# A six-block decoder on one core: the low-rank pieces ahead of ScalarE's transfers, and the second causal attention divided by GpSimd

## The chip, the core and the metric

The kernel runs on one core of a Trainium2 chip. The core has TensorE (PE in the profile; its weight loads are PEld), VectorE (DVE), ScalarE (ACT), GpSimd (POOL) and SyncE (SP), which here only starts transfers. ScalarE starts transfers as well, and each queue of transfers stands in line with what its engine does: a row marked ACTq or SPq is time of that engine's queue. The metric is the device time of one execution in microseconds, as a median of several runs; lower is better.

## The reference

The input is x of 8 batches x 128 tokens x 512 features, with a context of the same shape. Six blocks follow each other, and behind each one the result is added to x and layer-normalized:

```python
x = _layernorm(x + _L0_attn_ref(...))      # causal attention, 32 heads of 16
x = _layernorm(x + _L0_xattn_ref(...))     # autocorrelation with the context (FFT, top 9 lags)
x = _layernorm(x + _L0_ffn_ref(...))       # base matrix + low-rank experts, 2 of 28 by a router
x = _layernorm(x + _L1_attn_ref(...))      # causal attention with ALiBi, q and k layer-normalized
x = _layernorm(x + _L1_xattn_ref(...))     # cross attention: 16 heads of 96, 4 key heads
x = _layernorm(x + _L1_ffn_ref(...))       # 8 low-rank heads of rank 16, mixed by a softmax
```

The change touches the fourth block and the seam between the fifth and the sixth. The fourth, cut to what matters:

```python
qkv = jnp.clip(jnp.einsum('bsd,ed->bse', hidden_states, Wqkv), -8.0, 8.0)
q, k, v = jnp.split(qkv, [D_MODEL, 2 * D_MODEL], axis=-1)
q = _layer_norm(q, q_ln_w, q_ln_b)         # weights and biases over the 512 features
k = _layer_norm(k, k_ln_w, k_ln_b)
scores = jnp.einsum('bqhd,bkhd->bhqk', q, k) * scale + slopes * rel   # causal
probs = jax.nn.softmax(scores, axis=-1)
out = jnp.einsum('bhqk,bkhd->bqhd', probs, v)
return jnp.einsum('bsd,ed->bse', out, Wout)
```

The sixth block is `2 * sum over h of softmax(x Wr + br)[h] * 8 * (x A[h]) B[h]`.

## The kernel before

Everything is float32. Tokens of one batch stand on the 128 partitions; transposes that a product needs are made on TensorE against an identity. The program is written once as straight code. A planner then orders each engine's instructions: by their place in the program, but among those that by its own cost estimates are ready. So an instruction can run ahead of one written before it. `tc.issue_after` pins an order by hand. Waits between engines are put in by the framework.

**Second causal attention** (tiles named `..._a`, lines 164 to 240 and 600 to 860). The loop runs over the batches b, and in each over f = 0 and 2, half of the heads. One such step makes a `Heads16`: scores on TensorE (L164), the ALiBi bias and the maxima on VectorE (L672, L181), exponentials on ScalarE in two halves `exps(0)` and `exps(1)` (L193, each with its sum into `su`). The steps overlap three deep: while step n is scored, `turn` turns the exponentials of step n-1 on TensorE (`pt`, L212; copied by VectorE and ScalarE, L213), and `out` multiplies those of step n-2 with the values (L229, L235). The softmax's division is made at the end: `turn` takes the reciprocals of the sums (L202, `rc`), GpSimd spreads them over the features (L205, `rb`), TensorE turns them too (`pr`, L218), ScalarE copies them (`rT`, L220), and `out` multiplies its result with them on VectorE (L240). Beside that the next batch's q, k and v are made (`normed`, `values`): clipped and normalized by VectorE (L627, L631; the root of the variance by GpSimd, L97), multiplied by the norm's weights and raised by its biases on GpSimd (L632, L633), from `lnv`, four rows broadcast to all partitions whose q part is scaled once (L611). Then `turned_both` turns q (a VectorE copy, L137) and k (into `kbd`, which keeps two heads apart, L657).

**Cross attention and low-rank block** (tiles named `..._x`, lines 780 to 1150). Per batch there are two steps hh = 0, 1 of a `Heads8`: scores (L876), maxima, exponentials (L897), division and 32x32 transposes on VectorE (L904, L905), and then `turn`, 16 transfers from SBUF to SBUF that finish the transpose into `pT` (L911). `outputs(b)` multiplies with the values (`mixed`, L921) and `projected(b)` projects (L938) and normalizes. The pieces of the low-rank block run beside this: `low_tokens` (transposes of x), `low_scores` (products, L951, and the router's softmax, L960 to 973, with one exponential on ScalarE), `low_turn` (one transpose `pt_lT` on TensorE and one ScalarE copy `lT`, L1003 and L1006), `low_last` (a product `pof`, L1011, a normalization and the transfer of the output from SP, L1016). `nxt.go(n)` lets n pieces of the next pair's front part (token transposes, value products `pvx`, key products `pkx`, query products `pqx`) be issued.

For batches 0 to 5 all transfers of `turn` are started by SP. For the last two batches they are started together at the end of hh = 1, alternately by SP and ScalarE:

```python
                    pTs[b] = pT_tile(b)
                    for heads in (first, now):
                        heads.turn(pTs[b], (nc.sync, nc.scalar))
```

`pT` has one buffer, so these transfers wait until the values product of the batch before has read it. The buffers `e` of a `Heads8` are two, so the exponentials two steps later wait for the transfers that read the same buffer. The scores of one `Heads8` fill both pairs of PSUM banks in that pool, so the next scores wait for its exponentials.

Of the kernel before, what the change touches and what calls it, by code (L numbers as in the profile page):

```python
# [43 lines left out]
def decoder(ctx: ExitStack, tc: tile.TileContext, a: dict, out: bass.AP):  # L44
# [101 lines left out]
    class Heads16:  # L146
# [7 lines left out]

        W = 3 * P

        def __init__(self, pool, units, bias, o_dst, name, between=()):
            self.pool, self.units, self.o_dst, self.name = pool, units, o_dst, name
# [38 lines left out]

        def turn(self):


            rc = sm.tile([P, 16], F32, tag="rc", name=f"rc_{self.name}")
            nc.vector.reciprocal(rc, self.su.rearrange("p a r x -> p (a r x)"))  # L202

            rb = self.pool.tile([P, 2, 8, HD], F32, tag="rb", name=f"rb_{self.name}", bufs=1)
            nc.gpsimd.tensor_copy(rb, bc(rc.rearrange("p (a h) -> p a h", a=2).unsqueeze(3), [P, 2, 8, HD]))  # L205
            self.pT = self.pool.tile([P, 4, self.W], F32, tag="pT", name=f"pT_{self.name}", bufs=1)
            for i in range(2):
                pt = banks(f"pt_{self.name}_{i}")
                for r in range(2):
                    for k in range(3):  # L210
                        cols = slice(k * P, (k + 1) * P)
                        nc.tensor.transpose(pt[:, r, cols], self.e[:, 2 * i + r, cols], ident)  # L212
                (nc.scalar.copy if i else nc.vector.tensor_copy)(  # L213
                    self.pT[:, 2 * i : 2 * i + 2, :], pt[:, :, : self.W]
                )
            pr = bank(f"pr_{self.name}")
            for a in range(2):
                nc.tensor.transpose(pr[:, a * P : (a + 1) * P], rb[:, a].rearrange("p h d -> p (h d)"), ident)  # L218
            self.rT = self.pool.tile([P, 2, P], F32, tag="rT", name=f"rT_{self.name}", bufs=1)
            nc.scalar.copy(self.rT, pr[:, : 2 * P].rearrange("p (a q) -> p a q", a=2))  # L220

        def out(self):
            o = bank(f"o_{self.name}")
            for u, (_, _, v, vd) in enumerate(self.units):
# [9 lines left out]
                for r in range(4):  # L234
# [4 lines left out]
                    )  # L239
            nc.vector.tensor_tensor(  # L240
# [367 lines left out]
    lnv = kp.tile([P, 4, D], F32, tag="lnv", name="lnv")  # L608
    nc.sync.dma_start(lnv, a["L1_ln"].partition_broadcast(P))

    nc.gpsimd.tensor_scalar(lnv[:, 0:2, :], lnv[:, 0:2, :], SCALE, None, ALU.mult)  # L611
# [8 lines left out]
    def normed(i, b, xT, later=None):  # L620
# [9 lines left out]
        def normalized():  # L630
            done = nc.vector.tensor_scalar(q, q, mean, rs, ALU.subtract, ALU.mult)  # L631
            nc.gpsimd.tensor_tensor(q, q, lnv[:, 2 * i, :], ALU.mult)  # L632
            nc.gpsimd.tensor_tensor(q, q, lnv[:, 2 * i + 1, :], ALU.add)  # L633
# [16 lines left out]
    def turned_both(b, q, k):  # L650
        qT = ap.tile([P, NC, P], F32, tag="qT", name=f"qT1_{b}")
        transposed(q, NC, P, qT, f"qT1_{b}", "v")
# [5 lines left out]
        return qT, kbd  # L658
# [68 lines left out]
    qk = turned_both(0, *raw)  # L727
# [73 lines left out]
    for b in range(B):  # L801
# [3 lines left out]
        for f in (0, 2):  # L805
# [4 lines left out]
            now = Heads16(ap, units, alibi_bias(f), oT[:, f : f + 2, :], f"a1_{b}_{f}", keys_late)  # L810
            now.exps(0)
# [15 lines left out]
            if prev:  # L827
                prev.turn()
            now.exps(1)
            half = projection(b - 1, oT_before) if f == 2 and b else iter((0, 0))  # L830
            next(half)
            if b + 1 < B:
                if f == 0:
                    raw.append(normed(1, b + 1, xT, keys_late))
                else:
                    qk = turned_both(b + 1, *raw)
# [17 lines left out]
    with stage("x1b", 2, side="right") as ap, stage("f1", 2, side="right") as fp:  # L854
# [206 lines left out]
        for b in range(B):  # L1061
# [4 lines left out]
            for hh in range(2):  # L1066
# [4 lines left out]
                if b < B - 2 and hh == 0:  # L1071

                    nxt.go(3 if b < B - 3 else 2)
# [4 lines left out]
                elif b < B - 2:  # L1078
# [7 lines left out]
                    if b < B - 3:  # L1086
                        nxt.go(2)
# [7 lines left out]
                else:  # L1095
                    if b == B - 1:
                        low_turn(B - 4)
                        low_tokens(B - 3)
                    outputs(b - 1)
                    pTs[b] = pT_tile(b)  # L1100
                    for heads in (first, now):
                        heads.turn(pTs[b], (nc.sync, nc.scalar))
                    if b == B - 2:
                        low_turn(B - 5)
                        low_scores(B - 4)
                        low_last(B - 5)
            vs_x[b] = front.v[:, j]

        low_last(B - 4)
        projected(B - 2, {3: [lambda: low_scores(B - 3)]})  # L1110
        weight_sums()
        low_turn(B - 3)
        outputs(B - 1)
# [102 lines left out]
def _layouts(i):  # L1216
# [18 lines left out]
        ),  # L1235
        "L1_ln": np.stack([i[f"L1_attn_{k}"] for k in ("q_ln_w", "q_ln_b", "k_ln_w", "k_ln_b")]),
# [49 lines left out]
```

## Time and profile before

| what | value |
|---|---|
| median of 3 runs | 893.53 us (892.61 to 895.29) |
| the profiled execution | 892.05 us, its span 890.2 us |
| mean granted TensorE clock | 0.991 |
| busy: TensorE, VectorE, ScalarE, GpSimd | 852.1, 565.4, 362.0, 166.3 us |
| first causal attention and autocorrelation | to about 230 us |
| experts, beside the rest of the autocorrelation | to about 330 us |
| second causal attention | about 330 to 510 us |
| cross attention and low-rank block | about 510 to 890 us |

A row of the timeline gives start, duration, engine, line, operation, the tiles written and read, the shape, how many, and in brackets how long the engine had been idle and what ended that. A row of a group gives the busy time, the mean in ns, and the idle time ahead of it with the engines that ended it.

### The profile page before, as it was taken

What the parts mean: (1) busy time and instruction counts of PE and PEld (TensorE: products, weight loads), DVE (VectorE), ACT (ScalarE), POOL (GpSimd) and SP (SyncE); (2) the same over time, 40 slices, a digit from 0 to 9 for tenths busy, and PEclk for the clock granted to TensorE, in tenths of its full rate; (3) what the DMA queues carried; (4) which work ended last, traced back from release to release, by engine and by line L of the source; (5) the groups of instructions that cost most, each with busy time, mean ns of one, the idle gap of its engine ahead of it and who ended that gap; (6) DMA issues with size and microseconds to landing.
All of it is one profiled execution on the core that took longest, in us unless ns stands there. A gap on an engine that the chain in (4) does not pass through costs nothing.

```text
span 890.2 us, 16965 instructions
## 1 busy us (share of the span) xinstructions
PE 852.1 (96%) x6486; PEld 527.7 (59%) x6486; DVE 565.4 (64%) x1321; ACT 362.0 (41%) x1518; POOL 166.3 (19%) x235
## 2 busy tenths in 40 slices
PE   9999999899899999999999999999999999995996
PEld 5766655654455455555556687857485847582442
DVE  3756797786968667888888513724462546465644
ACT  3787474664223116666666502305030403053200
POOL 2500233132433313333333000000000000000000
PEclk9999999999999999999999999999999999998998
DMA  9800000130300002000004020432232222224040
GB/s 322 328 2 25 2 13 13 49 108 1 154 1 24 1 0 96 2 1 1 2 2 143 26 72 1 92 74 48 48 72 48 61 48 60 48 60 95 18 102 35
DMA packets 29921, 51.19 MB, mean 58 GB/s; under 512 B 5392, under 2 KB 21904, under 8 KB 27920
## 3 DMA queue, kind: packets, MB, share of 16 engines
q1 hardware_dynamic: 27280, 48.01, 18.1%
q10 hardware_dynamic: 2560, 2.10, 1.1%
q8 instruction: 51, 0.84, 0.4%
q14 instruction: 30, 0.25, 0.1%
HBM read 31.21 MB, written 2.10 MB: 37 GB/s over the span
## 4 chain that ended last, share of the span: by engine, by line
PE 68%; DVE 16%; ACT 9%; SPq 2%; issue 2%; ACTq 1%; POOL 1%; DMA 1%; POOLq 0%; DVEq 0%
PE pox L938 10%; PE pqx L86 6%; ACT e_a L193 5%; PE pq L86 5%; PE pkx L86 5%; PE pk L86 4%; PE pv L86 4%; PE pof L86 4%; PE o_x L921 3%; PE pt_a L212 3%; PE s_x L876 3%; PE pvx L86 3%; PE po L665 2%; PE s_a L164 2%; SPq L911 2%
## 5 line engine op out<-in xcount | busy, mean ns | idle before, releaser
L193 ACT ACTIVATE e_a<-e_a,m_a 128x128 f32<-128x128 f32 (+1 forms) x512 | 184.9, 365 | 113.8 <-DVE m_a L181 113.8
L897 ACT ACTIVATE e_x<-s_x,m_x 128x256 f32<-128x256 f32 x128 | 58.6, 483 | 135.8 <-DVE m_x L887 125.2
L193 ACT ACTIVATION_READ_ACCUMULATOR e_a<-e_a,m_a 128x1 f32 x512 | 97.6, 191 | 0.0
L938 PE MATMUL pox<-w_X_o,oTx 128*128 128x512 f32 x192 | 86.3, 604 | 0.0
L86 PE MATMUL pqx<-xTx,w_X_q 128*128 128x256 f32 x384 | 84.9, 380 | 0.0
L86 PEld LDWEIGHTS pqx<-xTx,w_X_q 128*128 128x128 f32 x384 | 72.6, 190 | 11.4 <-issue 1.8
L886 DVE TENSOR_REDUCE m_x<-s_x 128x4 f32<-128x1024 f32 x32 | 37.6, 1216 | 43.4 <-PE s_x L876 43.4
L938 PEld LDWEIGHTS pox<-w_X_o,oTx 128*128 128x128 f32 x192 | 36.6, 194 | 48.2 <-issue 47.7
L181 DVE TENSOR_REDUCE m_a<-e_a 128x4 f32<-128x512 f32 (+1 forms) x128 | 62.6, 543 | 0.0
L212 PE MATMUL pt_a<-ident,e_a 128*128 128x128 f32 x384 | 48.6, 274 | 4.9 <-DVE e_a L352 3.9
L212 PEld LDWEIGHTS pt_a<-ident,e_a 128*128 128x128 f32 x384 | 43.4, 140 | 12.8 <-DVE e_a L352 4.9
L97 POOL TENSOR_TENSOR rs_x<-ve_x,neghalf 128x1 f32<-128x1 f32 x7 | 3.8, 548 | 251.0 <-DVE ve_x L95 251.0
L876 PE MATMUL s_x<-kTx,qTx 32*128 32x256 f32 x768 | 46.1, 383 | 0.0
L921 PE MATMUL o_x<-pT_x,vx 128*32 128x512 f32 x384 | 43.3, 595 | 1.5 <-DVE oTx L927 1.4
L876 PEld LDWEIGHTS s_x<-kTx,qTx 32*128 32x128 f32 x768 | 38.1, 185 | 9.9 <-issue 7.4
L103 DVE TENSOR_TENSOR x_x<-pox,x_a 128x512 f32<-128x512 f32 x7 | 4.8, 692 | 56.5 <-PE pox L938 56.5
L905 DVE STREAM_TRANSPOSE e_x<-e_x 128x1024 f32<-128x1024 f32 x32 | 39.7, 1241 | 0.8
L904 DVE TENSOR_SCALAR e_x<-e_x,rc_x 128x256 f32<-128x256 f32 x128 | 36.4, 347 | 3.5 <-DVE rc_x L901 2.3
L164 PEld LDWEIGHTS s_a<-kbd,qT 32*64 32x64 f32 x1024 | 20.7, 131 | 28.1 <-issue 8.9
L792 ACT COPY qTx<-pqx 128x512 f32<-128x512 f32 x24 | 14.1, 594 | 55.5 <-PE pqx L86 55.5
L164 PE MATMUL s_a<-kbd,qT 32*64 32x256 f32 (+1 forms) x1024 | 33.3, 335 | 1.8 <-DVE pT_a L213 0.8
L202 DVE RECIPROCAL rc_a<-su_a 128x16 f32<-128x16 f32 x32 | 8.0, 251 | 40.6 <-ACT e_a L193 40.6
(222 smaller groups left out, 1637.7 us busy)
## 6 DMA issues: line engine op xcount, KB each, us to landing
pT_x<-e_x SPq DMA_DIRECT2D x224, 64.0 KB, 2.0
w_X_q<-in_X_q SPq DMA_DIRECT2D x3, 1024.0 KB, 4.8
w_X_o<-in_X_o SPq DMA_DIRECT2D x3, 1024.0 KB, 4.9
w_L_Wv<-in_L_Wv SPq DMA_DIRECT2D x2, 1024.0 KB, 6.4
w_L_Wo<-in_L_Wo SPq DMA_DIRECT2D x2, 1024.0 KB, 7.9
x_in<-in_x SPq DMA_DIRECT2D x8, 256.0 KB, 7.5
ct<-in_ctx SPq DMA_DIRECT2D x8, 256.0 KB, 4.4
cT<-in_ctxT SPq DMA_DIRECT2D x4, 512.0 KB, 3.9
```

What stands on the lines that cost most here:

```text
L86: nc.tensor.matmul(ps, lhsT=l, rhs=r, start=(i == 0), stop=(i == n - 1))
L164: nc.tensor.matmul(s[r // 2][64 * u : 64 * u + 64, r % 2, cols], lhsT=qT[rows, 64 - 64 * part : P - 64 * part], rhs=kbd[rows, :, :keys], s ...
L181: self.scored = nc.vector.tensor_reduce(self.m[:, part, rs, :], self.by_heads(part)[:, rs], AX.X, ALU.max, negate=True)
L193: nc.scalar.activation(e[:, r, x, :], e[:, r, x, :], AF.Exp, bias=self.m[:, part, r, x : x + 1], accum_out=self.su[:, part, r, x : x + 1],)
L212: nc.tensor.transpose(pt[:, r, cols], self.e[:, 2 * i + r, cols], ident)
L876: nc.tensor.matmul(sc[g // 2][:, g % 2, u * 256 : (u + 1) * 256], lhsT=qT[rows, (h0 + u) * NS + n, :], rhs=kT[rows, n], start=(n == 0), st ...
L886: nc.vector.tensor_reduce(m, self.s[i], AX.X, ALU.max, negate=True)
L897: nc.scalar.activation(self.e[:, :, j, :], self.s[half][:, i, :].rearrange("p (a k) -> p a k", k=32), AF.Exp, bias=self.m[:, j : j + 1], s ...
L904: nc.vector.tensor_scalar(e, e, self.rc[:, j : j + 1], None, ALU.mult)
L905: nc.vector.transpose(self.e[:, :, js, :], self.e[:, :, js, :])
L921: nc.tensor.matmul(po[32 * g : 32 * g + 32, :], lhsT=v[:, s, g * XD + 32 * n : g * XD + 32 * n + 32], rhs=pT[:, s].rearrange("p i h x -> p ...
L938: nc.tensor.matmul(po, lhsT=oT[:, n, h * P : (h + 1) * P], rhs=w, start=(i == 0), stop=(i == NX - 1))
```

## The change

1. In the second causal attention `divide(half)` takes the reciprocals of a half's sums as soon as its exponentials are made, and GpSimd multiplies the exponentials by them in place, before they are turned. The spread, the turn and the copy of the reciprocals leave `turn`; `out` copies instead of multiplying.
2. The norm of the queries is finished behind the transpose: ScalarE copies the turned queries feature by feature with the norm's weight as scale and its bias as addend. GpSimd's two operations on q go. The queries of the next batch are turned behind the scores of f = 2, the keys stay where they were. `lnv` keeps the keys' two rows, and `lnq` is a small tile for the queries.
3. In the last two batches the pieces of the low-rank block that stood behind the transfers, or behind the values product, are issued ahead of them. At the end `outputs(B - 1)` stands ahead of `low_turn(B - 3)`.
4. The front pieces of the even batches are shared out as 4 + 2 + 1 instead of 3 + 2 + 2.

```diff
+        def divide(self, half):
+            rs = slice(2 * half, 2 * half + 2)
+            if self.rc is None:
+                self.rc = sm.tile([P, 2, 4, 2], F32, tag="rcd", name=f"rc_{self.name}")
+            nc.vector.reciprocal(self.rc[:, :, rs, :], self.su[:, :, rs, :])
+            for part in range(2):
+                e = self.by_heads(part)[:, rs]
+                nc.gpsimd.tensor_tensor(e, e, bc(self.rc[:, part, rs, :].unsqueeze(3), list(e.shape)), ALU.mult)
+
         def turn(self):
-            rc = sm.tile([P, 16], F32, tag="rc", name=f"rc_{self.name}")
-            nc.vector.reciprocal(rc, self.su.rearrange("p a r x -> p (a r x)"))
...
+            if self.rc is None:
+                rc = sm.tile([P, 16], F32, tag="rc", name=f"rc_{self.name}")
...
+            if self.rc is not None:
+                return
             pr = bank(f"pr_{self.name}")
...
+            if self.rc is not None:
+                nc.vector.tensor_copy(self.o_dst, o[:, : 2 * P].rearrange("p (u q) -> p u q", u=2))
+                return
             nc.vector.tensor_tensor(
...
-    lnv = kp.tile([P, 4, D], F32, tag="lnv", name="lnv")
-    nc.sync.dma_start(lnv, a["L1_ln"].partition_broadcast(P))
-
-    nc.gpsimd.tensor_scalar(lnv[:, 0:2, :], lnv[:, 0:2, :], SCALE, None, ALU.mult)
+    lnv = kp.tile([P, 2, D], F32, tag="lnv", name="lnv")
+    nc.sync.dma_start(lnv, a["L1_ln"][2:4].partition_broadcast(P))
+    lnq = kp.tile([P, 2, NC], F32, tag="lnq", name="lnq")
+    nc.sync.dma_start(lnq, a["L1_lnq"])
+    nc.gpsimd.tensor_scalar(lnq, lnq, SCALE, None, ALU.mult)
...
-            nc.gpsimd.tensor_tensor(q, q, lnv[:, 2 * i, :], ALU.mult)
-            nc.gpsimd.tensor_tensor(q, q, lnv[:, 2 * i + 1, :], ALU.add)
+            if i:
+                nc.gpsimd.tensor_tensor(q, q, lnv[:, 0, :], ALU.mult)
+                nc.gpsimd.tensor_tensor(q, q, lnv[:, 1, :], ALU.add)
...
-    def turned_both(b, q, k):
+    def turned_queries(b, q):
         qT = ap.tile([P, NC, P], F32, tag="qT", name=f"qT1_{b}")
-        transposed(q, NC, P, qT, f"qT1_{b}", "v")
+        pt = bank(f"pTq1_{b}")
+        for c in range(NC):
+            nc.tensor.transpose(pt[:, c * P : (c + 1) * P], q[:, c * P : (c + 1) * P], ident)
+        for c in range(NC):
+            nc.scalar.activation(
+                qT[:, c, :], pt[:, c * P : (c + 1) * P], AF.Identity, scale=lnq[:, 0, c : c + 1], bias=lnq[:, 1, c : c + 1]
+            )
+        return qT
+
+    def turned_keys(b, k):
...
+            if f == 2 and b + 1 < B:
+
+                qT = turned_queries(b + 1, raw[0])
             now.exps(0)
             catch_up(now.scored)
...
+            now.divide(0)
             now.exps(1)
...
-                    qk = turned_both(b + 1, *raw)
+                    qk = qT, turned_keys(b + 1, raw[1])
+            now.divide(1)
...
-                    nxt.go(3 if b < B - 3 else 2)
+                    nxt.go((4, 3)[j] if b < B - 3 else 2)
...
-                        nxt.go(2)
+                        nxt.go((1, 2)[j])
...
                 else:
+                    low_turn(b - 3)
                     if b == B - 1:
-                        low_turn(B - 4)
                         low_tokens(B - 3)
                     outputs(b - 1)
+                    if b == B - 2:
+                        low_scores(B - 4)
+                    low_last(b - 3)
+
                     pTs[b] = pT_tile(b)
                     for heads in (first, now):
                         heads.turn(pTs[b], (nc.sync, nc.scalar))
-                    if b == B - 2:
-                        low_turn(B - 5)
-                        low_scores(B - 4)
-                        low_last(B - 5)
             vs_x[b] = front.v[:, j]
 
-        low_last(B - 4)
         projected(B - 2, {3: [lambda: low_scores(B - 3)]})
         weight_sums()
+        outputs(B - 1)
         low_turn(B - 3)
-        outputs(B - 1)
         low_tokens(B - 2)
         low_last(B - 3)
```

More of the change, by code (lines that the diff above doesn't have):

```diff
@@ L157, in __init__ @@
         def __init__(self, pool, units, bias, o_dst, name, between=()):
-            self.pool, self.units, self.o_dst, self.name = pool, units, o_dst, name
+            self.pool, self.units, self.o_dst, self.name, self.rc = pool, units, o_dst, name, None
             s = [banks(f"s_{name}_{i}") for i in range(2)]
@@ L196, in exps @@
                         )
-        def turn(self):
-            rc = sm.tile([P, 16], F32, tag="rc", name=f"rc_{self.name}")
-            nc.vector.reciprocal(rc, self.su.rearrange("p a r x -> p (a r x)"))
-            rb = self.pool.tile([P, 2, 8, HD], F32, tag="rb", name=f"rb_{self.name}", bufs=1)
-            nc.gpsimd.tensor_copy(rb, bc(rc.rearrange("p (a h) -> p a h", a=2).unsqueeze(3), [P, 2, 8, HD]))
+        def divide(self, half):
[6 more added lines that the diff above has]
+                nc.gpsimd.tensor_tensor(e, e, bc(self.rc[:, part, rs, :].unsqueeze(3), list(e.shape)), ALU.mult)
+        def turn(self):
+            if self.rc is None:
+                rc = sm.tile([P, 16], F32, tag="rc", name=f"rc_{self.name}")
+                nc.vector.reciprocal(rc, self.su.rearrange("p a r x -> p (a r x)"))
+                rb = self.pool.tile([P, 2, 8, HD], F32, tag="rb", name=f"rb_{self.name}", bufs=1)
+                nc.gpsimd.tensor_copy(rb, bc(rc.rearrange("p (a h) -> p a h", a=2).unsqueeze(3), [P, 2, 8, HD]))
             self.pT = self.pool.tile([P, 4, self.W], F32, tag="pT", name=f"pT_{self.name}", bufs=1)
@@ L657, in turned_both @@
         nc.vector.tensor_tensor(kbd, bc(pt.unsqueeze(1), [P, 2, D]), bc(pair.unsqueeze(2), [P, 2, D]), ALU.mult)
-        return qT, kbd
+        return kbd
     def projection(b, oT):
@@ L726, in decoder @@
     xT = turned_tokens(1)
-    qk = turned_both(0, *raw)
+    qk = turned_queries(0, raw[0]), turned_keys(0, raw[1])
     E(6)
@@ L1235, in _layouts @@
         ),
+        "L1_lnq": np.stack([cols(i[f"L1_attn_{k}"]) for k in ("q_ln_w", "q_ln_b")], axis=1),
         "L1_ln": np.stack([i[f"L1_attn_{k}"] for k in ("q_ln_w", "q_ln_b", "k_ln_w", "k_ln_b")]),
```

## The prediction

> **What bounds the kernel now.** I read the page's rows by slice first, then TensorE's waits over the last stage, then the timelines of TensorE and ScalarE around its one long wait, then the chain of waits in the second causal layer, and last the rows of single operations.
>
> ```profile
> PE   9999999899899999999999999999999999995996
> PEclk9999999999999999999999999999999999998998
> POOL 2500233132433313333333000000000000000000
> PE pof L1011 <- ACT lT L1006: 9.7, 2, 9.3
> PE o_x L921 <- DVE oTx L927: 1.4, 2, 0.7
> PE pt_lT L1003 <- DVE ve_x L95: 1.0, 1, 1.0
> ```
>
> TensorE (PE) is busy nearly everywhere. The dent in slice 37 is one wait of 9.3 us: the low-rank product of batch 3 (pof) waits for ScalarE's copy of the turned low-rank piece (lT).
>
> ```profile
> 808.47 2.87 PE L876 MATMUL s_x<-kTx,qTx 32*128 32x256 f32 x48
> 820.61 2.08 PE L1011 MATMUL pof<-wf,lT 128*128 128x512 f32 x2 [9.26 <-ACT lT L1006]
> 822.48 12.14 PE L938 MATMUL pox<-w_X_o,oTx 128*128 128x512 f32 x24
> 834.55 2.87 PE L876 MATMUL s_x<-kTx,qTx 32*128 32x256 f32 x48
> 808.96 11.21 ACTq L911 DMA_DIRECT2D pT_x<-e_x  x14
> 820.28 0.28 ACT L1006 ACTIVATE lT<-pt_lT 128x128 f32<-128x128 f32 x1 [11.44 <-DMA pT_x<-e_x]
> 837.77 0.28 ACT L1006 ACTIVATE lT<-pt_lT 128x128 f32<-128x128 f32 x1 [13.30 <-PE pt_lT L1003]
> ```
>
> The copy takes 0.28 us, but stands behind 16 transfers that ScalarE starts for batch 6 (807.42 to 820.17). The last line is the same copy one batch on: there low_turn stands ahead of the transfers in the program, and the copy runs 6 us before them (they start at 843.82).
>
> ```profile
> 401.53 1.31 PE pt_a L212 x12
> 402.84 0.22 PE pr_a L218 x2
> 403.05 3.44 PE pk L86 x8
> 406.49 0.84 PE s_a L164 x32
> ```
>
> In the second causal layer the chain of waits is TensorE without a gap, 21.79 us a batch (scores at 396.25 and 418.04); its two steps hold one pr_a each.
>
> **The change, part by part.** The sum is made against the profiled execution: 892.05 us, its span 890.2 and 1.85 around it; it lies 1.48 below the median of 893.53, and I carry the difference over to the median.
>
> (a) *Low-rank pieces of batches 6 and 7.* The transpose of batch 3's piece becomes possible when ls is made, at 788.2, so its copy can run before ScalarE's exponentials (804.6). TensorE then goes: batch 5's values to 807.4, pl, pof (0.86 warm) to 809.3, scores of batch 7 to 812.1, projection pox of batch 5 (10.5 warm) to 822.6. Before, pox ended at 834.6: 12.0 us gained, being 9.26 of waiting and 2.7 of half clock (pof 2.08 for 0.86, pox 11.95 for 10.5; the granted clock is 0.73 in 811.3 to 820.7 and 0.82 in 820.7 to 834.6).
> What is late next: the second scores of batch 7 need the PSUM of the first, so its exponentials, and these need the e buffer that the 16+16 transfers read. ScalarE's transfers still end at about 820.2 and the exponentials take 3.5 us (820.74 to 824.24): the scores start at 824.4, a new wait of 1.8 us. A 1.96 us gap at 110.6 left the clock at 1.00, so this one costs only itself. low_scores of batch 4 moves past ScalarE's transfers too: its exponential (0.5) needs a maximum that VectorE makes at 812.3. By readiness eight transfers go first, and it costs nothing that isn't covered; ahead of all of them it would hold them from 807.4 to 812.6, and the scores to 826.5, 2.1 lost. GpSimd is idle there (0.55 in 20 us), so the norm of x_f finds it free.
> After scores to 827.2 come transposes (0.7), o_x (5.3), pof (1.0), pox with pl (11.3), weight sums (0.9): TensorE is ready for the last values at 846.5. Their transfers start when batch 6's o_x is done (833.2), take 10.7 to issue and 2.0 to land: 845.9; low_last now also puts an output transfer on SP ahead of or among them, one issue of 0.65: 846.6. Taking 0.3 for collisions, 846.9 against 858.42: **11.5 gained**. The order outputs before low_turn at the end is in this: it hides the 1.04 us wait of pt_lT; the transpose then stands behind the values, which may cost 0.1. Part (a): **-11.4**.
>
> (b) *Front pieces, `go((4, 3)[j])`.* The sum over two batches stays 7+7. In even batches one value piece (2.6 us) comes ahead of the values product, whose waits for VectorE (0.73 at 626.4, 0.68 at 716.8) it covers; the key piece ahead of low_rank shifts VectorE's copies where 0.25 is lost now. No more than 1.66 us of TensorE idling exists there. I take **-1.2**, between -1.7 and +1.5.
>
> (c) *Second causal layer, TensorE.* Removed: two transposes pr_a in each of 16 turns, 0.22 each. In batch 0 the keys' transpose waits 0.97 for GpSimd and would wait 0.22 longer, so 15 count: -3.3. The moved query transposes are the same 0.44 a batch.
>
> (d) *The same layer, VectorE and ScalarE.* VectorE loses the copy of turned queries (L137, 0.69 a batch) just ahead of kbd, which today ends 0.3 before the scores that need it; that slack becomes about 1. It gets two small reciprocals for one (0.16 each by the 128x4 row L901, for 0.25) and a copy for the product of L240 (0.41 both). ScalarE loses rT (0.37 twice a batch) and gets four Identity copies, 0.28 to 0.46 each (L1006 and L337), 1.4 a batch, in its idle time of 4.4 before the exponentials of f = 2. Cost nothing; without that cover 0.7 a batch.
>
> (e) *GpSimd's division.* Nearest row: the in-place product with a broadcast reciprocal, L431.
>
> ```profile
> L431 POOL TENSOR_TENSOR ex<-ex,rcw 128x512 f32<-128x512 f32 x8 | 8.3, 1040 | 22.0 <-DVE rcw L430 18.5 <-DVE gx L582 3.4
> 235.57 1.10 DVE L580 TENSOR_SCALAR gx<-lg,topg 128x28 f32<-128x28 f32 x1
> 235.60 2.78 POOL L611 TENSOR_SCALAR lnv<-lnv 128x1024 f32<-128x1024 f32 x1
> 223.92 1.42 DVE L107 TENSOR_SCALAR x_a<-x_a,mv_a,rs_a 128x512 f32<-128x512 f32 x1 [0.66 <-POOL rs_a L97]
> ```
>
> So 1.04 for 512 columns and some 0.6 for 256: 3.3 a step, 6.6 a batch. Removed: rb (0.40 twice) and two products on q (1.27 each), 3.3 a batch; GpSimd goes from 8.2 to 11.5 of 21.4 us. The new wait is in turn: it needs the second half divided. In the step with f = 0, exps end at 406.9 and the transposes stand at 412.0; reciprocal and hops 0.5, products 1.6, an rs_k between 0.55: 2.6 of 5.1. In the other step 2.4 of 4.6. Queued behind the division on GpSimd are rs_q, rs_k and the products on k; k's run at 412.1 to 414.7, the halves are ready at about 403.4, 407.2, 414.5 and 418.2, so little collides, and rs_q may slip by 0.5.
> Now the rule that speaks against it. The rows show VectorE's scalar operations stretched while GpSimd works: 1.10 for a usual 0.23, and 1.42 for 0.55 beside memsets; copies out of PSUM stay the same (L213, 0.95). The Trainium skill, GPSIMD Engine Reference, section Key points, says that GpSimd shares its SBUF interfaces with VectorE and contends with instructions in a 2-port mode or with two SBUF inputs. Three instructions a batch are of the stretched kind (x, q, k normalized, 0.55 each), and today no GpSimd work overlaps them there. By the rows alone, with GpSimd idle at those moments, (c) stands at -3.3; by the rule, with q caught each time, q is 0.9 late against 0.3 of cover, 0.6 in each of 7 batches, and the layer ends at +0.9. The same rows bound it above if k is caught too: +5. x and k fall outside the ready times, q may fall inside: I take +1.0, so **-2.3 for the layer**, from -3.5 to +5.
>
> (f) *Norm vectors.* L611's 2.78 becomes a sliver of 8 columns. It stretches L580 by 0.9, behind which ScalarE's wT copy and then pw wait (1.11). I take **-0.5** (-1.2 to +1, if the small extra load lands late and holds GpSimd).
>
> Sum: -11.4 - 1.2 - 2.3 - 0.5 = -15.4: 876.6 for the profiled execution, **878.1** for the median.
>
> **The rivals.**
> *SP's queue takes the wait over.* low_last also starts the output's transfer on SP, now ahead of the 16 that SP issues. If it stands first in the queue, these wait for x_f. In batch 6 x_f is ready at about 815.6 instead of transfers from 807.4: the exponentials start at 822.8, the scores at 826.5. In batch 7 x_f comes 6.9 us after o_x (850.6 against 843.75 today), so 841.7, and the transfers land at 854.1, a wait of some 6 us, which by the clock rows above costs 2.6 more. Then (a) gives 1.7 and the time is 887.8. Against it: the planner orders by readiness (the reciprocal L202 runs ahead of the earlier-written bias), and the first transfers are ready 3 us before the output.
> *The piece is not moved.* The planner may leave lT's copy behind the transfers; then only (b), (c) to (f) act: 889.5. Against it is the batch-7 line above.
> *Slower: GpSimd becomes the bound of the second causal layer.* Its other work there is 2.5 us a step. At three times the row, the products are 9.8, a step is 12.3 instead of 10.9, and 16 steps cost 23: with (a), (b) and (f) the end is 903.6. It decides from 2.8 times the row (9.2 us of products a step), where it cancels the rest. For it: contention is in the trace. Against: GpSimd's worst stretch there is its 0.40 copy at 0.86.
>
> **How the numbers follow.** Forecast 0.70 (873.5 to 883), SP's queue 0.13 (883 to 891), not moved 0.08, GpSimd bound 0.06, unlisted gains or losses 0.03. About 0.3%, 2.7 us, is what a measurement of this kernel can tell from no change. Faster: 0.70 + 0.13 + 0.05 of not moved + 0.02 = 0.90; within: 0.04; slower: 0.06. The range 873.5 to 888.5 leaves out the upper part of the SP case (0.04), not moved, GpSimd (0.14) and 0.02 below.
>
> **What the profile should show.** Right: pof of batch 3 within 1 us of pl, with no 9 us wait on lT; scores of batch 7 waiting 1 to 3 us on exponentials; granted clock 1.00 until the last 10 us; no pr_a or rT in the second layer, a batch of about 21.4 us there, GpSimd at 11 to 13. Wrong: SP's transfers of batch 6 or 7 starting after an output transfer; pt_a of the second layer waiting on GpSimd; normalized q stretched to over 1 us with TensorE waiting for its transpose; or a wait over 4 us ahead of the last values.

## The result, and the profile after

The changed kernel is slower: 903.83 us (903.04 to 904.61, 4 runs) against 893.85 us (892.61 to 895.29, 4 runs) of the kernel before on the same chip, a ratio of 1.0121 with a 95% interval of 1.0105 to 1.0136. The forecast was 878.1, with a range of 873.5 to 888.5. (The quotient of the two medians is 1.0112; ratios here are those on record, estimated from the runs of both kernels.) The profiled execution has a span of 902.3 us against 890.2, and the mean granted clock is 0.991 in both. So by the medians 10.0 us are lost. The traces have 12.1 to account for, because the profiled execution of the kernel before was a fast one.

The dent that the forecast started from is gone, and GpSimd's row shows where the work went. Slices of the changed kernel's page:

```profile
PE   9999999999899999999999999999999999999796
...
POOL 2401233132323304445554300000000000000000
PEclk9999999999999999999999999999999999999998
```

TensorE's waits over the whole span (time in total, times, longest) tell more. Those of the two edited stages in the changed kernel:

```profile
PE s_a L165 <- DVE kbd L686: 10.9, 6, 1.9
...
PE pt_xTf L129 <- DVE x_x L107: 3.8, 1, 3.8
...
PE pTq L674 <- DVE q L650: 1.8, 6, 0.3
...
PE o_x L955 <- DMA pT_x<-e_x: 1.4, 1, 1.4
```

The 9.7 us on lT have left the list. In their place stand six waits of 1.8 us for kbd, a new one of 3.8 us for x_x, and one of 1.4 us for the last transfers. TensorE never waits for the divided exponentials in the second causal layer.

To see where the time went, I set the starts of the same TensorE instructions in both traces against each other and took how far the changed kernel is behind at each stage's end. The difference over each stage, forecast beside measured:

| stage | forecast | changed kernel |
|---|---|---|
| up to the first scores of the second causal layer | -0.5 (f) | +0.7 |
| second causal layer | -2.3 (c to e) | +12.5 |
| cross attention, to the values of batch 5 | -1.2 (b) | +3.5 |
| from there to the end | -11.4 (a) | -4.6 |

Three of four parts are wrong by 4.7 us or more. The +0.7 of the first row is not the work of the edit: TensorE's clock was granted at 0.50 from 176.3 to 179.7 us in the trace of the changed kernel, and at 1.00 there in that of the kernel before. The starts on either side put its cost at 1.0 us. Both kernels have the same instructions up to there: such a spell can stand in one execution and not in another.

Now the largest. VectorE's timeline (start, duration, operation, and in brackets the idle time before it), first in the kernel before, then at the same place in the changed kernel:

```profile
415.92 0.69 DVE L137 COPY qT<-pt_qT 128x512 f32<-128x512 f32 x1 [1.23 <-PE pt_qT L129]
416.53 1.21 DVE L657 TENSOR_TENSOR kbd<-pTk,masks 128x1024 f32<-128x1024 f32 x1
418.61 0.25 DVE L202 RECIPROCAL rc_a<-su_a 128x16 f32<-128x16 f32 x1 [0.86 <-ACT e_a L193]
```

```profile
419.69 0.91 DVE L224 COPY pT_a<-pt_a 128x768 f32<-128x768 f32 x1
423.61 0.20 DVE L203 RECIPROCAL rc_a<-su_a 128x8 f32<-128x8 f32 x1 [3.01 <-ACT e_a L194]
423.73 1.17 DVE L686 TENSOR_TENSOR kbd<-pTk,masks 128x1024 f32<-128x1024 f32 x1
```

And TensorE's in the changed kernel, in the same microseconds:

```profile
420.78 0.60 PE L684 MATMUL pTk<-ident,k 128*128 128x128 f32 x4
421.22 1.88 PE L694 MATMUL po<-w_L_Wo,oT 128*128 128x512 f32 x4
424.95 0.91 PE L165 MATMUL s_a<-kbd,qT 32*64 32x256 f32 x32 [1.85 <-DVE kbd L686]
```

The turned keys (pTk) are there at 421.4. VectorE could make kbd then. It idles for 3.0 us instead, because the next instruction in its queue is the reciprocal of `divide(1)`, which needs the last of ScalarE's exponentials. Behind that reciprocal of 0.20 us stands kbd, and behind kbd stand the scores. In the program `divide(1)` is written behind the keys; the planner put its reciprocal ahead of them. A batch of the layer takes 23.83 us instead of 21.79. (Behind the last of the six waits the clock is at half from 497.1 to 500.5. From the scores there to the layer's end it is 29.4 us, and 28.9 in the first experiment's kernel, whose clock is full there. So I estimate the half clock at 0.5 of the 12.5 us.)

### The profile page after: what moved, and what is told of

Its sections match the earlier page's. It is cut to its first block, busy times and chain, and to the rows that moved or that the text cites. A ratio compares the mean times of both kernels' runs of the same rounds, so it can differ in the third digit from the quotient of the medians.

```text
span 902.3 us, 16968 instructions
## 1 busy us (share of the span) xinstructions
PE 855.9 (95%) x6454; PEld 526.2 (58%) x6454; DVE 563.4 (62%) x1329; ACT 370.2 (41%) x1534; POOL 188.7 (21%) x267
## 4 chain that ended last, share of the span: by engine, by line
PE 63%; DVE 20%; ACT 10%; POOL 2%; DMA 2%; issue 2%; SPq 1%; POOLq 0%; DVEq 0%; ACTq 0%
PE pqx L86 9%; ACT e_a L194 7%; PE pox L972 7%; PE pvx L86 5%; PE o_x L955 4%; PE pkx L86 4%; PE s_x L910 4%; PE pof L86 4%; PE pq L86 3%; PE pk L86 3%; PE pv L86 3%; DVE e_a L701 3%; DVE m_a L182 2%; PE s_a L165 2%; PE pt_a L223 2%
## 5 line engine op out<-in xcount | busy, mean ns | idle before, releaser
L206 POOL TENSOR_TENSOR e_a<-e_a,rc_a 128x512 f32<-128x512 f32 x64 | 51.8, 826 | 44.2 <-DVE rc_a L203 20.1
L910 PE MATMUL s_x<-kTx,qTx 32*128 32x256 f32 x768 | 50.0, 385 | 1.0 <-ACT e_x L931 1.0
L955 PE MATMUL o_x<-pT_x,vx 128*32 128x512 f32 x384 | 45.4, 615 | 2.6 <-DMA pT_x<-e_x 1.4
```

Of the source, the lines that this page charges most:

```text
L206: nc.gpsimd.tensor_tensor(e, e, bc(self.rc[:, part, rs, :].unsqueeze(3), list(e.shape)), ALU.mult)
L910: nc.tensor.matmul(sc[g // 2][:, g % 2, u * 256 : (u + 1) * 256], lhsT=qT[rows, (h0 + u) * NS + n, :], rhs=kT[rows, n], start=(n == 0), st ...
L955: nc.tensor.matmul(po[32 * g : 32 * g + 32, :], lhsT=v[:, s, g * XD + 32 * n : g * XD + 32 * n + 32], rhs=pT[:, s].rearrange("p i h x -> p ...
```

## Experiments

The theory to be tested, R: the layer's loss is the place of one small reciprocal in VectorE's queue. The rival, G: GpSimd's division holds the layer, as a bound or by stretching VectorE. For the end of the kernel the first theory, X, was that VectorE's norm of x_x comes late. The first four kernels were made to part these.

### One edge: the reciprocal behind kbd

The changed kernel, with:

```diff
-            nc.vector.reciprocal(self.rc[:, :, rs, :], self.su[:, :, rs, :])
+            with tc.issue_after(behind.ins) if behind else nullcontext():
+                nc.vector.reciprocal(self.rc[:, :, rs, :], self.su[:, :, rs, :])
...
-            now.divide(1)
+            now.divide(1, turned_keys.done if f == 2 and b + 1 < B else None)
```

> The changed kernel with one edge more: in the steps with f = 2 the second small reciprocal of the division is queued on VectorE behind kbd, the masked keys of the next batch, instead of ahead of it. Theory R (the reciprocal holds kbd in VectorE's queue until ScalarE's exponentials are done, and the next scores with it): six gaps of 1.84 us ahead of the scores s_a go, so about 11 us less than the changed kernel's 903.8: 892 to 893, and a batch of the layer takes about 21.9 us instead of 23.83. Theory G (the layer is held by GpSimd: its division, or VectorE stretched beside it): the order on VectorE is of no account, 902 to 904, a batch stays at 23.5 or more.

Measured: 893.97 us, ratio to the kernel before 1.0012 (1.0004 to 1.002), where the changed kernel had 1.0121. That is 1 us above R's range and far from G's. One instruction of 0.20 us a batch, moved behind its neighbor, is worth 1.1%, about 10 us. VectorE's queue now has kbd first, and the scores' wait for it is gone:

```profile
440.87 1.23 DVE L687 TENSOR_TENSOR kbd<-pTk,masks 128x1024 f32<-128x1024 f32 x1 [0.84 <-PE pTk L685]
443.05 0.20 DVE L204 RECIPROCAL rc_a<-su_a 128x8 f32<-128x8 f32 x1 [0.95 <-ACT e_a L194]
```

R holds for these 10 us, G does not: the division on GpSimd is the same in both kernels. But the layer still takes 2.0 us more than before, where the forecast had 2.3 less, and a batch 22.2 us. The longest of TensorE's waits in the layer, 1.8 us in all in the changed kernel, names what is left:

```profile
PE pTq L675 <- DVE q L651: 3.2, 6, 0.6
```

### The division alone

The kernel before, with `divide` and what belongs to it, and with the queries handled as before.

```diff
+            now.divide(0)
             now.exps(1)
...
+            now.divide(1)
```

> The kernel before with GpSimd's division alone; the queries are turned, normalized and copied as before (VectorE's copy of the turned queries stays, GpSimd keeps their two products), the low-rank pieces and the front's pieces stay. With that copy in VectorE's queue the second reciprocal stands behind kbd. Theory R: the fifteen pairs of pr_a go (-3.3 us), some contention comes back (+1): 891 to 893 against 893.9 before. Theory G: GpSimd carries most here, 3.3 us of products a step beside the 2.5 of q and the rest; the layer loses what the changed kernel loses there or more: 904 to 910.

Measured: 897.3 us, ratio 1.0054 (1.0034 to 1.0075): between the two expectations. By the trace's starts the layer alone costs 5.6 us. The wait for kbd is not there, since the second reciprocal stands behind kbd in this kernel. Another one is:

```profile
PE pTk L671 <- POOL k L649: 5.8, 6, 2.6
```

GpSimd's timeline in one batch shows why:

```profile
414.73 1.27 POOL L648 TENSOR_TENSOR q<-q,lnv 128x512 f32<-128x512 f32 x1 [0.36 <-DVE q L647]
415.96 1.04 POOL L206 TENSOR_TENSOR e_a<-e_a,rc_a 128x512 f32<-128x512 f32 x1
416.96 1.27 POOL L649 TENSOR_TENSOR q<-q,lnv 128x512 f32<-128x512 f32 x1
418.19 0.61 POOL L206 TENSOR_TENSOR e_a<-e_a,rc_a 128x256 f32<-128x256 f32 x1
418.76 0.55 POOL L97 TENSOR_TENSOR rs_k<-ve_k,neghalf 128x1 f32<-128x1 f32 x1
```

GpSimd is not the bound by its busy time. But the small rs_k, for which the keys wait, stands behind 4.2 us of products. The keys come late, and their transpose on TensorE waits 0.6 us a batch, 2.6 in the first, where it was 1.0 before. Behind that wait of 2.6 the clock is at half for a time (0.82 on average from 346.5 to 360.3, where the kernel before has 1.00). From the keys' transpose to the second scores behind it, it is 13.6 us against 11.1 before, so I estimate the half clock at 2.5 of the 5.6 us in this trace, which is of the slowest of this kernel's five executions. So G is right for this kernel, as a matter of the queue; the changed kernel escapes it by taking q's two products off GpSimd.

### The queries alone

The kernel before, with `turned_queries` on ScalarE behind the scores of f = 2, and the division by the reciprocals' rows as before.

```diff
+            if f == 2 and b + 1 < B:
+                qT = turned_queries(b + 1, raw[0])
             now.exps(0)
...
-                    qk = turned_both(b + 1, *raw)
+                    qk = qT, turned_keys(b + 1, raw[1])
```

> The kernel before with the queries' part alone (norm weights applied by four Identity copies on ScalarE, the query transposes moved behind the scores of f = 2); the division stays as before, by the reciprocals' rows. Without VectorE's copy of the turned queries the one reciprocal of a step stands ahead of kbd in VectorE's queue here as well. Theory R: it waits for all the exponentials, kbd behind it, and the scores behind that: about 2 us in each of six batches, 904 to 907. Theory G (no division on GpSimd, which also loses two products a batch): no loss, 892 to 894.

Measured: 902.05 us, ratio 1.011 (1.0094 to 1.0126). R had 904 to 907, G no loss. No work of the division is in this kernel, and it loses almost what the changed kernel loses. Its wait, and the two rows behind it:

```profile
PE s_a L164 <- DVE kbd L670: 9.0, 6, 2.4
```

```profile
423.29 0.25 DVE L202 RECIPROCAL rc_a<-su_a 128x16 f32<-128x16 f32 x1 [3.69 <-ACT e_a L193]
423.46 1.16 DVE L670 TENSOR_TENSOR kbd<-pTk,masks 128x1024 f32<-128x1024 f32 x1
```

Here it is the one old reciprocal, whose line was not edited, that stands ahead of kbd. Put side by side, the orders on VectorE say what tips it. Where VectorE copies the turned queries (before, and the division alone) its queue runs copy, kbd, reciprocal. Where that copy is gone (the changed kernel, and the queries alone) it runs reciprocal, kbd. So the "saved" 0.69 us of VectorE work goes with a loss of 10 us. What tips the planner was not tested: the queries' part also moves TensorE's transposes and adds ScalarE's copies. That the planner takes the reciprocal for ready too early is my reading of its order.

### The root of q's variance ahead of the products

The changed kernel with the first edge, and one more on GpSimd:

```diff
+            with tc.issue_after(power.ins) if power else nullcontext():
+                for part in range(2):
...
-            now.divide(0)
+            now.divide(0, power=moments.power if f == 0 and b + 1 < B else None)
```

> The changed kernel with the reciprocal behind kbd as in the first experiment, and with one edge more: in the steps with f = 0, GpSimd's products of the first half are queued behind the small power that the normalized queries wait for (rs_q). Theory Q (what is left of the layer's loss is that power, 0.12 us long, standing behind a product of 1.04): six gaps of 0.6 ahead of the queries' transpose go: 889.5 to 891 against 893.97 with the first edge alone, a batch takes about 21.5 instead of 22.2. Theory C (the stretched normalization beside GpSimd's product, 0.83 for 0.55, is the loss): the product only comes later and meets it all the same; less than 1 us is gained, 893 to 894.

(The power takes 0.55 us by its row, not 0.12 as the expectation says.) Measured: 890.81 us, ratio 0.9983 (0.9975 to 0.9991), by the ratios 2.6 us less than with the first edge alone, as Q has it. The wait is gone, and the layer now ends 0.65 us earlier than before, a batch at about 21.65. The normalization of q, with the first edge alone:

```profile
430.95 0.83 DVE L651 TENSOR_SCALAR q<-q,mv_q,rs_q 128x512 f32<-128x512 f32 x1 [1.62 <-POOL rs_q L97]
```

and with both edges:

```profile
405.89 1.25 DVE L652 TENSOR_SCALAR q<-q,mv_q,rs_q 128x512 f32<-128x512 f32 x1 [0.66 <-POOL rs_q L97]
```

Both theories have a part. Waiting for rs_q falls from 1.62 to 0.66, as Q says. The normalization takes 1.25 instead of 0.83, as C says. In both kernels it starts 0.07 us behind the start of one of GpSimd's products and ends 0.28 us behind that product's end, in each of the six batches. With the first edge alone it meets the product of 256 columns (0.61), with both edges the one of 512 (1.04). So it looks less like a slowdown than like a wait for the product that began first. The wait for rs_q shrinks by more, so 0.5 us a batch is won.

Most of what is missing from the prediction's gain of 3.3 went into this: the moved transposes of q wait about 0.1 for the normalization and take 0.58 to the next group's start instead of 0.43, and the first batch's keys wait 1.4 us for GpSimd, where it was 1.0.

### The front's pieces alone

```diff
-                    nxt.go(3 if b < B - 3 else 2)
+                    nxt.go((4, 3)[j] if b < B - 3 else 2)
...
-                        nxt.go(2)
+                        nxt.go((1, 2)[j])
```

> The kernel before with the front's pieces alone (four and three pieces ahead of the mixing, one and two behind). Theory of the prediction: the value piece covers waits of the values product in even batches: -1.2 (-1.7 to +1.5), 891.5 to 894. Theory S (in the changed kernel the second half's scores of batches 2 and 4 come in pieces between the values products, and the start of the last stages lies 3.5 us later against the start of cross attention): 895.5 to 897.5 against about 893.3 before.

Measured: 896.02 us, ratio 1.004 (1.0024 to 1.0056); by the trace's starts cross attention loses 2.8 us. TensorE's timeline in batch 2 of the loop:

```profile
626.93 1.92 PE L921 MATMUL o_x<-pT_x,vx 128*32 128x512 f32 x16
628.78 0.70 PE L876 MATMUL s_x<-kTx,qTx 32*128 32x256 f32 x4
629.67 1.92 PE L921 MATMUL o_x<-pT_x,vx 128*32 128x512 f32 x16 [0.18 <-DVE oTx L927]
631.52 0.70 PE L876 MATMUL s_x<-kTx,qTx 32*128 32x256 f32 x4
632.35 1.92 PE L921 MATMUL o_x<-pT_x,vx 128*32 128x512 f32 x16
634.20 0.70 PE L876 MATMUL s_x<-kTx,qTx 32*128 32x256 f32 x4
634.96 10.57 PE L938 MATMUL pox<-w_X_o,oTx 128*128 128x512 f32 x24
645.45 2.43 PE L876 MATMUL s_x<-kTx,qTx 32*128 32x256 f32 x36
```

The same stretch in the kernel before:

```profile
622.71 3.64 PE L921 MATMUL o_x<-pT_x,vx 128*32 128x512 f32 x32
627.08 1.92 PE L921 MATMUL o_x<-pT_x,vx 128*32 128x512 f32 x16 [0.73 <-DVE oTx L927]
628.94 10.57 PE L938 MATMUL pox<-w_X_o,oTx 128*128 128x512 f32 x24
639.43 2.87 PE L876 MATMUL s_x<-kTx,qTx 32*128 32x256 f32 x48
```

The wait of 0.73 is covered, as forecast. But the planner fills it with four scores at a time. 48 scores in one group take 2.87 us; in four groups they take 3 x 0.70 + 2.43 = 4.53: each time the group is split, some 0.55 is added. From the first values to the end of the scores it is 20.95 us against 19.59: 1.4 lost in batch 2, and 1.7 in batch 4 in the same way. Theory S holds.

### The low-rank part alone

```diff
+                    low_turn(b - 3)
                     if b == B - 1:
-                        low_turn(B - 4)
                         low_tokens(B - 3)
                     outputs(b - 1)
+                    if b == B - 2:
+                        low_scores(B - 4)
+                    low_last(b - 3)
...
```

> The kernel before with the low-rank part alone (the pieces ahead of the last transfers, and the order of the last pieces). Theory of the prediction: the 9.3 us wait and the half clock behind it go, nothing of size comes for it: -11.4, 882 to 883. Theory X (what is late next is VectorE's add for x_x of batch 5, queued behind the exponentials' work of batch 7, so that the transposes for the low-rank piece and the values behind them on TensorE come 3.8 us late, and the last values wait for their transfers again): -4 to -6, 888 to 890.

Measured: 888.74 us, ratio 0.9963 (0.995 to 0.9977): by the medians 4.1 us where the forecast had 11.4, as X has it. TensorE's timeline in the last stage, from batch 5's projection on:

```profile
815.43 10.57 PE L938 MATMUL pox<-w_X_o,oTx 128*128 128x512 f32 x24
...
833.83 1.11 PE L129 MATMUL pt_xTf<-ident,x_x 128*128 128x128 f32 x4 [3.41 <-DVE x_x L107]
834.87 7.90 PE L921 MATMUL o_x<-pT_x,vx 128*32 128x512 f32 x48
...
857.54 5.36 PE L921 MATMUL o_x<-pT_x,vx 128*32 128x512 f32 x48 [1.56 <-DMA pT_x<-e_x]
```

The projection ends at 826.0 and starts 10.2 us earlier against the rest than before. But VectorE adds it to x only at 830.71, behind the division and transposes of batch 7's first exponentials, and the values of batch 6 stand behind the transposes that wait for it. The wait costs more than its 3.41 us. Behind it the clock is granted at 0.50 from 833.2 to 840.0, and the values of batch 6 take 7.90 us where those of batch 7 take 5.36 at full clock. The changed kernel has the same: 3.79 us of waiting, half clock from 848.7 to 852.1, and 7.05 us for these values. Two kernels move that add.

### The norm of x_x between, or ahead of, the exponentials' work

Both are the low-rank part with `projected(5)` written ahead, and an edge that queues the second half of the exponentials' work (first kernel) or both halves (second kernel) behind its norm:

```diff
                 now.exps(0)
-                now.exps(1)
+                if b == B - 1 and hh == 0:
+                    projected(b - 2)
+                with tc.issue_after(add_norm.done.ins) if b == B - 1 and hh == 0 else nullcontext():
+                    now.exps(1)
```

> The kernel before with the low-rank part, and with the add and norm of x_x of batch 5 queued on VectorE between the two halves of the exponentials' work of batch 7's first heads, instead of behind both. Theory X: x_x is ready 2.7 us earlier, the wait of 3.4 us ahead of the low-rank transposes falls to 0.7, and the end comes 2.5 to 4 us earlier than with the low-rank part alone (888.7): 885 to 886. Rival T (the last values wait for their transfers, which end when they end): TensorE waits for the transfers instead, less than 1 us is gained.

> As the kernel before this in the list, but with the add and norm of x_x of batch 5 ahead of both halves of the exponentials' work. Theory X: the wait of 3.4 us is gone, but the exponentials' work of batch 7 ends 1 to 3 us later and with it the maxima of the second heads; 884.5 to 886. Rival T: the exponentials that were held now set when the last transfers start, and the time is 887 or more.

Measured: 889.77 us, ratio 0.9967 (0.9957 to 0.9976), and 890.79 us, ratio 0.9976 (0.9963 to 0.9988). Neither is faster than the low-rank part alone. In the first the wait for x_x falls from 3.4 to 0.9 us, the values of batch 6 run at full clock (5.36 us), and the projection of batch 6 starts 5.2 us earlier. All of it is given back in one place:

```profile
PE pt_xTf L129 <- DVE x_x L107: 0.9, 1, 0.9
...
855.27 8.03 PE L921 MATMUL o_x<-pT_x,vx 128*32 128x512 f32 x48 [4.84 <-DMA pT_x<-e_x]
```

The last values wait 4.8 us for their transfers, and the half clock (0.50 from 853.9 to 860.7) now falls on them: 8.03 us instead of 5.36. Rival T holds. X was true of the wait and false of the time. Which transfers, the queue of SP says (start, time in the queue, how many), in the first of these kernels:

```profile
837.28 4.44 SPq L911 DMA_DIRECT2D pT_x<-e_x  x7
846.61 0.34 SPq L1016 DMA_DIRECT2D out<-x_f  x1
847.00 6.51 SPq L911 DMA_DIRECT2D pT_x<-e_x  x9
```

Seven of SP's sixteen transfers go out, then SP does nothing from 841.7 to 846.6: next in its queue is the output of the low-rank piece, and that waits for the norm of x_f, which VectorE ends at 846.59. Nine transfers stand behind it. ScalarE's sixteen are all out at 849.6, SP's at 853.5.

### The output transfer behind SP's sixteen

The first of these two kernels, with the transfer of the output issued on SP behind the last transfer of `turn`; then the same without the moved norm.

```diff
-                    low_last(b - 3)
+                    y = add_norm(xs[b - 3], low_sum(b - 3, turned_lows.pop(b - 3)), f"f1_{b - 3}")
...
                         heads.turn(pTs[b], (nc.sync, nc.scalar))
+                    with tc.issue_after(now.sent.ins):
+                        nc.sync.dma_start(out[b - 3], y)
```

> The kernel before with the low-rank part, the norm of x_x between the two halves as in the kernel of run e7_norm_half, and the output transfer of the low-rank piece queued on SP behind the sixteen transfers of the last two batches instead of among them. Theory SP (the first rival of the prediction, in batch 7 only: nine of SP's transfers stand behind an output transfer that waits for x_f until 846.6, while ScalarE's sixteen are out at 849.6): SP's last transfers go out about 3 us earlier, TensorE's wait of 4.8 us ahead of the last values falls to 1 to 2.5, the time to 886 to 887.5 (889.8 without it). Theory B (ScalarE's transfers or the landing set the moment): the wait stays over 4 us, 889 to 890.

> The kernel before with the low-rank part and the output transfer behind SP's sixteen, the norm of x_x left behind the exponentials' work. If the output transfer among SP's sixteen is most of what the low-rank part loses again: 885 to 886.5. If the late norm (3.4 us ahead of the low-rank transposes) holds the values of batch 6 and through them the last transfers all the same, which is what the page of the low-rank part alone shows first: 887.5 to 889.

Measured: with the moved norm 884.14 us, ratio 0.9898 (0.9882 to 0.9914); without it 887.82 us, ratio 0.9951 (0.9935 to 0.9968). SP's queue and the wait of the last values in the first of them:

```profile
834.40 12.15 SPq L911 DMA_DIRECT2D pT_x<-e_x  x16
846.69 0.48 SPq L1111 DMA_DIRECT2D out<-x_f  x1
```

```profile
849.38 5.36 PE L923 MATMUL o_x<-pT_x,vx 128*32 128x512 f32 x48 [1.84 <-DMA out<-x_f]
```

The row names the transfer of the output as what ended the wait. The values don't read it, and the profile infers such releasers, so which transfer came last here is open. The wait falls as theory SP has it, by 3.0 us, but the time falls by 5.6. The rest fits the clock: it is granted at 1.00 behind this shorter wait, and the last values take 5.36 us instead of 8.03. Without the moved norm the wait of 3.4 us for x_x is still there, with half clock behind it (0.50 from 830.5 to 837.3), as the second of that kernel's expectations says.

So the low-rank part loses again at two waits, one behind the other, with half clock behind each where it is long. Against the kernel before, the low-rank part alone is at -3.7 per mille. Moving the late norm alone leaves it at -3.3, moving the output transfer alone at -4.9; both intervals overlap that of the low-rank part alone. Both together give -10.2. With both, the stage from the values of batch 5 to the end gains 9.8 us; the forecast's part (a) had 11.4.

### All parts, mended

The changed kernel with both edges of the layer, the moved norm, the output behind SP's sixteen, and the front's pieces as before.

> The changed kernel with the reciprocal behind kbd, the products behind rs_q, the norm of x_x between the halves, the output transfer behind SP's sixteen, and the front's pieces as before. If the parts add: 890.8 (both edges), less 3.5 for the front's pieces, less 0.5 to 3.5 for the norm and the output transfer: 883.5 to 887. If the front's pieces cost nothing next to the other parts, 887 to 890.

Measured: 885.44 us, ratio 0.9914 (0.9896 to 0.9931). This is what the parts add up to. But it is not faster than the low-rank part so mended by itself (0.9898); the intervals of the two overlap. The division and the queries bring 0.6 us by their stage's trace, less than the intervals can tell. The lowest ratio here is that of the kernel before with the mended low-rank part alone, 1.0% faster than the kernel before.

## Why the prediction was wrong, point by point

The forecast was -15.4 us, and the traces have +12.1. Of the 27.5 between, 14.8 lie in the second causal layer (10.5 of them in one queue), 6.8 in part (a), 4.7 in part (b) and 1.2 in the stage of part (f).

**(d) VectorE and ScalarE, "Cost nothing": the step that failed most, and without which the change would have been within 0.2% of the kernel before.** It counted VectorE's work and asked nothing of its order. Of the copy of turned queries it said that it stands just ahead of kbd and that its going widens kbd's slack to about 1. The reciprocal took its place. The prediction held the numbers that price this: part (e) lists the halves of the exponentials as ready at 403.4, 407.2, 414.5 and 418.2, and the chain of waits had the scores at 418.04. A reciprocal that needs the half of 418.2, ahead of the kbd that scores at 418.04 need, cannot be free. Measured by the kernel that puts it behind kbd, this is 9.9 us of 10.0 by the medians, and 10.5 of 12.1 by the traces. The forecast asked nothing about what is queued behind this wait on its engine.

**(e) GpSimd's division: the cover was right, the charge too small.** The products took what the row L431 gave, 1.04 us for 512 columns, and pt_a never waited for them. The stretch of VectorE's work beside GpSimd's, weighed there with the rule of the Trainium skill (GPSIMD Engine Reference, section Key points) that GpSimd and VectorE share their SBUF interfaces, is in the runs: q's normalization takes 0.55 before, 0.79 on average in the changed kernel and 1.25 where it meets the product of 512 columns. But +1.0 was taken. With the first edge the layer is at +2.0 against a sum of -2.3. Most of the 4.3 between was not the stretch: rs_q stood behind a product of 1.04 (the text allowed it "0.5"), and one edge took 2.6 of it away, the longer normalization included. The rest lies for the most part in the moved transposes and the first batch.

**(c) The two transposes** are gone, 0.22 each, but with both edges the layer gains only 0.65 us, not 3.3. The 0.44 a batch was saved on TensorE and mostly paid back ahead of and in the moved transposes of q, which (c) took to cost "the same".

**(a) The low-rank pieces: mechanism right, later waits missed.** The 9.26 us and the half clock behind them went as forecast: pox of batch 5 comes about 10 us earlier. "What is late next" was sought in the scores of batch 7 and in the e buffer, at 1.8 us; they waited 1.0 in the changed kernel. Late next were VectorE's norm of x_x and the output transfer in SP's queue. In the changed kernel's trace the first costs 3.8 us of waiting and 1.7 of half clock, and the last values then wait 1.4 for their transfers: 6.9 together, about the 6.8 that are missing. The sum put x_x at nothing.

The output transfer is the forecast's first rival. It stood among SP's sixteen in batch 6 too, but the scores behind it waited no more than 1.0 us there. In batch 7 it counted. The main sum charged it "one issue of 0.65", while the rival with the full price was given 0.13. That rival also priced the half clock behind its wait, at 2.6; behind the wait of 4.8 us it was 2.7. With both mended the part gives 9.8.

**(b) The front's pieces:** the covered waits were right, the sign wrong. Splitting the scores was not thought of; the part costs 2.8 us on its own and 3.5 in the changed kernel, outside the range of -1.7 to +1.5.

**(f) The norm vectors:** right. Beside the shorter GpSimd operation VectorE's gx takes 0.25 us where it took 1.10, in the changed kernel and in the four others with this edit:

```profile
236.75 0.25 DVE L596 TENSOR_SCALAR gx<-lg,topg 128x28 f32<-128x28 f32 x1
238.19 1.13 PE L461 MATMUL pw<-wT,dft 128*128 128x512 f32 x2 [0.68 <-ACT wT L139]
```

TensorE's wait for wT falls from 1.11 to 0.68. (In the kernel with the division alone the old, longer operation starts 0.6 us behind gx and leaves it at 0.23.) The stage from the last scores of the first causal layer to the first of the second takes 125.8 us in four traces with the edit and at full clock. It takes 126.25 in the two kernels without it whose clock was full there and whose wait just ahead (pg, 1.65) is the same. That is -0.45, where -0.5 was forecast. The kernel before has 125.8 as well, because that wait ahead was 1.18 in its trace.

**The slower rival** gave 903.6 (its own terms sum to about 903.4), and 903.83 was measured. It was right by accident. It asked for products of at least 2.8 times their row, and they took 1.0 times.

## What to carry to other kernels

An instruction of 0.2 us that waits is as long as its wait for everything behind it in its engine's queue: for each wait that a change adds, and for each instruction that it removes, write down the engine's order and compare the ready time of the waiting one with the due time of the next. Where a planner sets the order, removing work can move an unedited instruction; pin it by hand. And when a wait is taken away, follow its gain to the next one and the one after: of two waits in series, mending either alone showed next to nothing here. Look at the granted clock behind each wait as well. Between the values of batch 5 and those of batch 7, the waits of 3.4 us and more all had half clock behind them here, and those of 1.4 to 1.9 none.

## What the runs showed that I had not expected

- VectorE's 128x512 normalization takes 0.55 us alone. Where it starts 0.07 us behind one of GpSimd's in-place products, it ends 0.28 us behind that product's end: 0.83 us in all beside a product of 0.61, and 1.25 beside one of 1.04. The product keeps its time. In the kernel with both edges the next one, of 256 columns, takes 0.80 instead of 0.61.
- Scores of 48 packed instructions take 2.87 us in one group and 4.53 split into 4 + 4 + 4 + 36.
- Executions drift where nothing was edited. With the instructions of the kernel before up to the second causal layer, the low-rank part's profiled execution reached the layer 3.1 us later. It had two spells of half clock on the way, 113.0 to 116.4 and 239.3 to 242.7, that the kernel before has not. The other traces have none, one or two of them, each within 1.5 us of a wait of 0.7 to 2.0 us that all traces have, and are 0.2 us earlier to 3.2 later. So the forecast's remark that the gap of 1.96 us at 110.6 left the clock at 1.00 holds for its own trace, but not for five others. A gain of one stage has to be read from that stage's own start, and its clock looked at.
